# Perceiver kernel: which batches get their keys and values made ahead, and row chains moved to VectorE

## The chip, the cores and the metric

The kernel runs on one core of one Trainium2 chip. The metric is the device time of one execution in microseconds (us); three runs of the kernel before took 1544.31, 1554.78 and 1555.05 us, the median is 1554.78 us.

## What is computed

Two layers over x of 16 batches x 64 rows x 256 columns, all in 32-bit floating point. Each batch also has a context of 1024 positions x 256. Cut to what matters (layer norms have no weights):

```
x = x + cross_attention_0(layernorm(x), ctx)       # 16 heads of 16, keys and values from ctx
x = x + column_attention(layernorm(x))             # across the 16 batches, rotary, softmax with +1
x = x + mixture_of_experts(layernorm(x))           # 8 experts, the best 2, capacity 256
x = x + cross_attention_1(layernorm(x), ctx) + out_b   # with a bias per context position and a mask
x = x + row_attention(layernorm(x)) @ w_proj + b_proj  # among the 64 rows of a batch, rotary
x = x + fp4_linear(silu(fp4_linear(n, w_gate)) * fp4_linear(n, w_up), w_down),  n = layernorm(x)
```

`fp4_linear` rounds both operands, in blocks of 16 along the contracted dimension, to a grid of eight magnitudes: the block's scale is the largest absolute value over 6.

## The kernel before

Rows are held as eight tiles `x[n]` of 128 rows (two batches each). TensorE's order is written out by hand (`manual_schedule`); the order on the other engines and on the DMA queues is set by a scheduler from the dependences and the place in the program.

**Cross-attention** (L307 to L625) runs through 64 *slots* `(b, dt, hf)`: batch b, one of two groups of eight heads, one of two halves of the 1024 keys. At step i of the loop at L590, TensorE does the scores of slot i + 2 (L445, four PSUM banks), then the steps of `project` that are due (L597), the 16 transposes of slot i's exponentials (L475), and the products with the values of slot i - 1 (L489). VectorE adds the mask and takes the minimum (L456), ACT takes the exponential (L467), and both copy the transposes back (L217, L219). PSUM has seven banks for this and one for the output. Between two groups of transposes `advance` (L553) takes every open *row chain* one `yield` further: a chain is a Python generator that does the finishing of a batch (`outputs`, L497, with `project_rows`, L297) and then, in the second layer, `row_attention` (L1220) and `feed_forward` (L1361) of a row tile. A `yield` so decides how much of the other work lies between two steps of a chain in TensorE's order. The queries of the next tile (`queries`, L394) are such a chain too.

**Keys and values** of a batch come from eight steps of `project` (L361): four for the keys (L370), four for the values (L385). In the second layer nine batches, 0 to 8 (`AHEAD = 9`), have them made ahead: `make_ahead` (L636) does the eight steps during the first layer's column attention and experts, where `fill` calls for them, and stores them to DRAM (`kd`, `vd`); the second layer loads them (`load_keys`, L346). The others are projected in the second layer. `due` (L542) places their steps: two in each of the slots 4b - 4 to 4b - 1, or, where the batches on both sides are made ahead (`alone`), one in each of the slots 4b - 6 to 4b + 1. With batches 0 to 8 made ahead no batch is `alone`.

**Layer norm of a row tile** (`layernorm_rows`, L241): statistics, the variance and a first guess of its inverse root are made on VectorE (L244 to L253), three Newton steps of three instructions each on 128x1 and the normalization itself (L256 to L260) on POOL. `project_rows` adds the bias on VectorE (L303) and the sum to `x[n]` on POOL (L304).

**`fp4`** (L883): ACT takes absolute values (L890), VectorE the largest of each block (L893), scales, rounds by adding and subtracting a large power of two, and scales back (L894 to L911). `feed_forward` makes gate and up in two halves of 352 columns (L1376, L1379, L1380), quantizes both halves, transposes (L1391) and multiplies by the down weights (L1405). The last row tile goes through the same steps with nothing beside it.

Of the kernel before, what the change touches and what calls it, by code (L numbers as in the profile page):

```python
# [19 lines left out]
P = 128  # L20
# [7 lines left out]
AHEAD = 9  # L28
# [90 lines left out]
def kernel(ctx: ExitStack, tc: tile.TileContext, a: dict, out: bass.AP):  # L119
# [121 lines left out]
    def layernorm_rows(pool, n, name="xnr"):  # L241

        st = small.tile([P, 6], F32, name="bnst")
        nc.vector.bn_stats(st, x[n])  # L244
        mv = small.tile([P, 2], F32, name="mvr")
        nc.vector.bn_aggr(mv, st)
        va = small.tile([P, 1], F32, name="var")
        nc.vector.tensor_scalar(va, mv[:, 1:2], EPS, None, ALU.add)

        half = small.tile([P, 1], I32, name="half")  # L250
        nc.vector.tensor_scalar(half, va.bitcast(I32), 1, None, ALU.logical_shift_right)
        r = small.tile([P, 1], F32, name="rsd")
        nc.vector.tensor_scalar(r.bitcast(I32), half, -1.0, 1597463007.0, ALU.mult, ALU.add)  # L253
        t = small.tile([P, 1], F32, name="nwt")
        for _ in range(3):
            nc.gpsimd.tensor_scalar(t, r, va, r, ALU.mult, ALU.mult)  # L256
            nc.gpsimd.tensor_scalar(t, t, -0.5, 1.5, ALU.mult, ALU.add)
            nc.gpsimd.tensor_tensor(r, r, t, ALU.mult)
        xn = pool.tile([P, D], F32, name=name)
        made[name] = nc.gpsimd.tensor_scalar(xn, x[n], mv[:, 0:1], r, ALU.subtract, ALU.mult)  # L260
        yield
        yield
        yield
        return xn
# [32 lines left out]
    def project_rows(n, oT, w, bias):  # L297

        pm = bank()
        for c in range(KC):  # L300
            nc.tensor.matmul(pm[:, :D], oT[:, c, :], w[:, c, :], start=(c == 0), stop=(c == KC - 1))  # L301
        t = small.tile([P, D], F32, name="prow")
        nc.vector.tensor_tensor(t, pm[:, :D], bias, ALU.add)  # L303
        nc.gpsimd.tensor_tensor(x[n], x[n], t, ALU.add)  # L304


    def cross_attention(layer, wq, wkv, wo, bq, bk, bv, bo, mask, keep, bias, after, ready, arrive, idle):  # L307
        side = "right" if layer else "left"
        with ExitStack() as st:
# [84 lines left out]
            def queries(n):  # L394
# [3 lines left out]
                xn = yield from layernorm_rows(single, n, "xnq")  # L398
# [98 lines left out]
            def outputs(b):  # L497
# [38 lines left out]
                project_rows(n, oT, wo, rowbias(bo))  # L536
# [99 lines left out]
    def make_ahead(b):  # L636
# [3 lines left out]
        for step in range(8):  # L640
# [27 lines left out]
            if step == 7:  # L668
                load_ahead(b + 2)
# [4 lines left out]
    def load_ahead(b, put=nc.sync.dma_start):  # L674
        if b < AHEAD:
            actx[b] = ahead.tile([P, KC, SK], F32, name="actx")
            put(actx[b], a["ctxT"][b].rearrange("(c p) k -> p c k", p=P))
# [3 lines left out]
    ahead_steps = (None for b in range(AHEAD) for _ in make_ahead(b))  # L681
# [201 lines left out]
    def fp4(pool, dst, src, rows, n, tag, most=None):  # L883

        nb = n // BLK
        most = most or n
        shape = [rows, nb, BLK]
        t = pool.tile([P, most], F32, name=f"t{tag}")[:rows, :n]
        t3 = t.rearrange("p (g k) -> p g k", k=BLK)
        nc.scalar.activation(t, src, AF.Abs)  # L890
        yield
        scl = pool.tile([P, most // BLK], F32, name=f"scl{tag}")[:rows, :nb]
        nc.vector.tensor_reduce(scl, t3, AX.X, ALU.max)  # L893
        nc.vector.tensor_scalar(scl, scl, 1.0 / 6.0, 1e-12, ALU.mult, ALU.max)  # L894
        rsc = pool.tile([P, most // BLK], F32, name=f"rsc{tag}")[:rows, :nb]
# [4 lines left out]
            t3, src.rearrange("p (g k) -> p g k", k=BLK), rsc.unsqueeze(2).to_broadcast(shape), ALU.mult  # L900
# [4 lines left out]
        m = pool.tile([P, most], F32, name=f"m{tag}")[:rows, :n]  # L905
# [257 lines left out]
    def quantize_weights(step, pool):  # L1163
        if step < 4:
# [9 lines left out]
            for _ in fp4(pool, q, raw, PG, n, "w"):  # L1174
                pass
# [11 lines left out]
        elif step < 6:  # L1187
# [4 lines left out]
            for _ in fp4(pool, q, raw, P, NI, "d"):  # L1192
                pass
# [14 lines left out]
    def last_layers(one):  # L1208
# [11 lines left out]
        def row_attention(n, two):  # L1220
            vz = vzs[n % 2]
            xn = yield from layernorm_rows(two, n)
# [134 lines left out]
            project_rows(n, oT, wproj, rowbias("L1_attn_b_proj"))  # L1357
# [3 lines left out]
        def feed_forward(n, two):  # L1361
            tok = slice(n * P, (n + 1) * P)
            xn = yield from layernorm_rows(two, n)
            yield from fp4(one, xn, xn, P, D, "h", NI)
# [5 lines left out]
            for g in range(2):  # L1370
                cols = slice(g * NH, (g + 1) * NH)
                pg = bank()[:, :NH]
                pu = bank()[:, :NH]
                for ps, w in ((pg, wgT), (pu, wuT)):
                    for c in range(KC):
                        nc.tensor.matmul(  # L1376
                            ps, xT[:, c, :], w[:, c, cols], start=(c == 0), stop=(c == KC - 1)
                        )
                nc.scalar.activation(h[:, cols], pg, AF.Silu)  # L1379
                nc.vector.tensor_tensor(h[:, cols], pu, h[:, cols], ALU.mult)  # L1380
            yield
            for g in range(2):
                cols = slice(g * NH, (g + 1) * NH)
                yield from fp4(one, h[:, cols], h[:, cols], P, NH, "h", NI)
            yield
            hT = one.tile([P, NCH, P], F32, name="hT")
            for g in range(0, NCH, 3):
# [12 lines left out]
            yield  # L1400
            yield
            py = bank()[:, :D]
            for j in range(NCH):
                w = min(P, NI - j * P)
                nc.tensor.matmul(py, hT[:w, j, :], wdT[:w, j, :], start=(j == 0), stop=(j == NCH - 1))  # L1405
# [13 lines left out]
    with first_layer:  # L1419
# [11 lines left out]
        with (  # L1431
# [19 lines left out]
            fill(8 * AHEAD)  # L1451
# [61 lines left out]
```

## Time and profile before

| | us |
|---|---|
| runs: lowest, median, highest | 1544.31, 1554.78, 1555.05 |
| profiled execution, its own time | 1553.52 |
| its span, first to last instruction | 1551.8 |
| TensorE busy in the span | 1411.0 (91%) |
| VectorE, ACT, POOL busy | 880.4 (57%), 725.3 (47%), 285.4 (18%) |
| mean granted TensorE clock | 0.942 |

In the lines of the timeline each row has the start in us, the duration in us, engine, line of the kernel, operation, output <- input, the shapes, and in brackets the idle time of the engine before it and what ended that. In the rows of waits: total us, times, longest. In the rows by stage: the stage, its length, busy us (instructions) of TensorE, of its weight loads, of VectorE, ACT and POOL, then the granted TensorE clock as a share of full speed, the DMA engines' mean share, and GB/s. Busy times of TensorE are modelled: instructions overlap, so a busy TensorE is not one at its peak.

### The profile page before, as it was taken

The page shows a single profiled execution, that of the slowest core. Times are in us where ns is not written, and L with a number is a line of the kernel's source. Part 1 is how long each engine was busy: PE and PEld are TensorE (multiplying, and loading weights), DVE is VectorE, ACT ScalarE, POOL GpSimd, SP SyncE. Part 2 cuts the span into 40 slices and gives each one's busy share as a digit, 9 for nine tenths or more (in the row PEclk, how much of TensorE's full clock was granted, in tenths as well). Part 3 has the DMA queues.
Part 4 walks back from the last instruction along what each step waited for, and adds up shares of the span by engine and source line. Part 5 has one row for each costly group of instructions (what it writes and reads, how often), then busy time and mean ns, then how long its engine had stood idle before and what let it go on. Part 6 is the DMA issues. An engine that isn't in the chain of part 4 may idle for free.

```text
span 1551.8 us, 32601 instructions
## 1 busy us (share of the span) xinstructions
PE 1411.0 (91%) x13488; PEld 995.0 (64%) x13488; DVE 880.4 (57%) x2325; ACT 725.3 (47%) x1339; POOL 285.4 (18%) x502
## 2 busy tenths in 40 slices
PE   4999999999999998999999787888899999999754
PEld 2667766676667655768887555565657666666542
DVE  2556665656565533365721265675767675757543
ACT  2555555555555532223221475564656465646321
POOL 4101010000000031013300134241414141311111
PEclk8999999999999999999999798888889999999876
DMA  8111110101000021377774232322101111100000
GB/s 281 59 31 35 32 59 32 35 32 59 31 28 2 35 90 70 105 260 235 234 283 147 90 117 94 118 86 74 57 14 46 46 52 49 42 5 1 5 5 3
DMA packets 53073, 119.48 MB, mean 77 GB/s; under 512 B 4877, under 2 KB 24333, under 8 KB 50621
## 3 DMA queue, kind: packets, MB, share of 16 engines
q1 hardware_dynamic: 48876, 109.93, 21.0%
q0 software_dynamic: 1648, 4.72, 1.1%
q10 hardware_dynamic: 2400, 2.76, 0.5%
q8 instruction: 106, 1.74, 0.5%
q14 instruction: 43, 0.34, 0.1%
HBM read 94.32 MB, written 23.07 MB: 76 GB/s over the span
## 4 chain that ended last, share of the span: by engine, by line
PE 73%; DVE 12%; POOL 4%; ACT 4%; DMA 3%; issue 3%; ACTq 0%; POOLq 0%; DVEq 0%; SPq 0%
PE psw L475 11%; PE psw L385 10%; PE psw L370 9%; PE psw L445 8%; PE pso L489 7%; PE psw L659 4%; PE psw L1085 4%; PE psw L1105 4%; DVE e L456 3%; PE psw L646 3%; ACT e L467 3%; PE psw L1376 2%; PE psw L1405 2%; PE psw L301 2%; DMA kd<-astage 1%
## 5 line engine op out<-in xcount | busy, mean ns | idle before, releaser
L467 ACT ACTIVATE e<-e,mn 128x1024 f32<-128x1024 f32 x256 | 291.1, 1139 | 125.3 <-DVE mn L456 125.3
L475 PEld LDWEIGHTS psw<-consts,e 128*128 128x128 f32 x2048 | 242.6, 144 | 111.6 <-issue 64.3
L475 PE MATMUL psw<-consts,e 128*128 128x128 f32 x2048 | 286.8, 280 | 10.1 <-DVE mn L456 5.7
L456 DVE CUSTOM_DVE_ANT_0 e<-psw,negb,mn 128x512 f32<-128x512 f32 x256 | 177.9, 747 | 180.0 <-PE psw L445 180.0
L456 DVE CUSTOM_DVE_ANT_0 e<-psw,negb 128x512 f32<-128x512 f32 x256 | 162.9, 686 | 87.0 <-PE psw L445 86.8
L219 ACT COPY eT<-psw 128x512 f32<-128x512 f32 x320 | 174.1, 590 | 58.3 <-PE psw L475 57.9
L445 PE MATMUL psw<-kT,qm 32*128 32x512 f32 x1024 | 167.7, 690 | 3.4 <-ACT qm L415 1.8
L489 PE MATMUL pso<-eT,v 128*32 128x128 f32 x4096 | 146.0, 286 | 0.0
L370 PE MATMUL psw<-ctxT,w_L_xattn_Wkv 128*128 128x512 f32 x256 | 125.0, 612 | 11.9 <-DMA ctxT<-in_ctxT_dram 11.9
L217 DVE COPY eT<-psw 128x512 f32<-128x512 f32 x192 | 123.0, 678 | 9.3 <-PE psw L475 9.3
L489 PEld LDWEIGHTS pso<-eT,v 128*32 128x32 f32 x4096 | 109.4, 114 | 28.0 <-issue 25.9
L385 PE MATMUL psw<-w_L_xattn_Wkv,ctxT 128*128 128x256 f32 x512 | 123.6, 385 | 0.0
L385 PEld LDWEIGHTS psw<-w_L_xattn_Wkv,ctxT 128*128 128x128 f32 x512 | 93.0, 190 | 33.7 <-issue 11.9
L370 PEld LDWEIGHTS psw<-ctxT,w_L_xattn_Wkv 128*128 128x128 f32 x256 | 44.3, 192 | 68.4 <-issue 55.1
L219 ACT COPY v<-psw 128x512 f32<-128x512 f32 x46 | 27.0, 588 | 123.8 <-PE psw L385 123.8
L304 POOL TENSOR_TENSOR x<-x,prow 128x256 f32<-128x256 f32 x24 | 17.4, 727 | 315.1 <-DVE prow L303 315.1
L659 PE MATMUL psw<-w_L_xattn_Wkv_w,actx 128*128 128x256 f32 x288 | 73.4, 409 | 0.8 <-ACT astage L653 0.8
L445 PEld LDWEIGHTS psw<-kT,qm 32*128 32x128 f32 x1024 | 49.2, 197 | 37.8 <-issue 20.2
L337 POOL TENSOR_SCALAR negb<-m 128x1024 f32<-128x1024 uint8 x16 | 16.7, 1046 | 285.8 <-DVE mn L456 172.4
L380 ACT ACTIVATE kT<-psw,colb 128x512 f32<-128x512 f32 x48 | 32.8, 687 | 75.3 <-PE psw L370 75.3
L646 PE MATMUL psw<-actx,w_L_xattn_Wkv_w 128*128 128x512 f32 x144 | 66.2, 599 | 1.3 <-DVE x L632 1.3
L659 PEld LDWEIGHTS psw<-w_L_xattn_Wkv_w,actx 128*128 128x128 f32 x288 | 58.0, 206 | 13.6 <-issue 3.8
(248 smaller groups left out, 1974.0 us busy)
## 6 DMA issues: line engine op xcount, KB each, us to landing
ctxT<-in_ctxT_dram SPq DMA_DIRECT2D x23, 1024.0 KB, 5.0
w<-in_L_ffn_w_dram SPq DMA_DIRECT2D x16, 1024.0 KB, 6.9
actx<-in_ctxT_dram SPq DMA_DIRECT2D x9, 1024.0 KB, 6.8
kd<-astage SPq DMA_DIRECT2D x36, 256.0 KB, 3.7
vd<-astage SPq DMA_DIRECT2D x36, 256.0 KB, 2.4
kT<-kd SPq DMA_DIRECT2D x9, 1024.0 KB, 6.1
v<-vd SPq DMA_DIRECT2D x9, 1024.0 KB, 5.0
ab<-in_fside_BxS_dram SPq DMA_DIRECT2D x32, 256.0 KB, 3.4
```

What stands on the lines that cost most here:

```text
L217: nc.vector.tensor_copy(dst, src)
L219: nc.scalar.copy(dst, src)
L370: nc.tensor.matmul(pm, wkv[:, c, dt * P : (dt + 1) * P], ctxT[b][:, c, cols], start=(c == 0), stop=(c == KC - 1),)
L385: nc.tensor.matmul(pm[:, j * D : (j + 1) * D], ctxT[b][:, c, (k + j) * P : (k + j + 1) * P], wkv[:, c, D : 2 * D], start=(c == 0), stop=(c ...
L445: nc.tensor.matmul(sc[g], qm[b // 2][r : r + 32, dt, b % 2, :, :].rearrange("p j q -> p (j q)"), kT[b][r : r + 32, dt, cols], start=True, ...
L456: nc.vector.tensor_tensor_reduce(out=e[:, cols], in0=sc[g], in1=negb[b][:, cols], scale=1.0, scalar=3e38 if hf == 0 else mn[b][:, 0, pr : ...
L467: nc.scalar.activation(e, e, AF.Exp, scale=-1.0, bias=mn[b][:, 1, pr : pr + 1], accum_out=sums[b][:, pr : pr + 1])
L475: nc.tensor.transpose(pt[:, g * P : (g + 1) * P], es[b, dt, g][:, k * P : (k + 1) * P], ident)
L489: nc.tensor.matmul(po[b][32 * g : 32 * g + 32, dt, :], v[b][:, k, pr * 32 : (pr + 1) * 32], e[:, g, :], start=(k == 0), stop=(k == NK - 1),)
L646: nc.tensor.matmul(pm, w1kv[:, c, dt * P : (dt + 1) * P], actx[b][:, c, cols], start=(c == 0), stop=(c == KC - 1),)
L659: nc.tensor.matmul(pm[:, j * D : (j + 1) * D], actx[b][:, c, (k + j) * P : (k + j + 1) * P], w1kv[:, c, D : 2 * D], start=(c == 0), stop=( ...
L1085: nc.tensor.matmul(ph[:, j * CAP : (j + 1) * CAP], w1[:, c, (f + j) * P : (f + j + 1) * P], xeT[:, c, :], start=(c == 0), stop=(c == KC - 1),)
```

## The change

- `AHEAD` lists the nine batches made ahead: 0, 1, 2, 4, 6, 8, 10, 12, 14. So 3, 5, 7, 9, 11, 13 and 15 are projected in the second layer, and each is `alone`. Loads and stores follow the list.
- `layernorm_rows` can do the Newton steps and the normalization on VectorE (two tiny instructions a step instead of three, and one ahead). `row_attention`, `feed_forward` and the first queries of the second layer use that; the other queries stay on POOL. With the argument set, it has no `yield`s of its own.
- In the second layer `x[n]` gets the bias of the coming projection on POOL as soon as it has been normalized, and `project_rows` adds the product to it in one instruction on VectorE.
- `fp4` leaves out the pass on ACT; the maximum takes absolute values itself. Its tiles come from the caller.
- `feed_forward` works in columns 0 to 383 and 384 to 703, with more `yield`s between its steps. For the last row tile there are none, and the second part's gate and up stand behind the first part's scaling; transposes and down products of the first part stand ahead of the quantization of the second.

```diff
-AHEAD = 9
+AHEAD = (0, 1, 2, 4, 6, 8, 10, 12, 14)
...
-    def layernorm_rows(pool, n, name="xnr"):
+    def layernorm_rows(pool, n, name="xnr", vector=False):
...
+        xn = pool.tile([P, D], F32, name=name)
+        if vector:
+            nc.vector.tensor_scalar(va, va, -0.5, None, ALU.mult)
+            for _ in range(3):
+                nc.vector.tensor_scalar(t, r, va, r, ALU.mult, ALU.mult)
+                nc.vector.scalar_tensor_tensor(r, t, 1.5, r, ALU.add, ALU.mult)
+            made[name] = nc.vector.tensor_scalar(xn, x[n], mv[:, 0:1], r, ALU.subtract, ALU.mult)
+            return xn
         for _ in range(3):
             nc.gpsimd.tensor_scalar(t, r, va, r, ALU.mult, ALU.mult)
...
-    def project_rows(n, oT, w, bias):
+    def project_rows(n, oT, w, bias=None):
...
+        if bias is None:
+            nc.vector.tensor_tensor(x[n], pm[:, :D], x[n], ALU.add)
+            return
...
-                xn = yield from layernorm_rows(single, n, "xnq")
+                xn = yield from layernorm_rows(single, n, "xnq", layer == 1 and n == 0)
+                if layer:
+                    nc.gpsimd.tensor_tensor(x[n], x[n], rowbias(bo), ALU.add)
...
-                project_rows(n, oT, wo, rowbias(bo))
+                project_rows(n, oT, wo, None if layer else rowbias(bo))
...
-    ahead_steps = (None for b in range(AHEAD) for _ in make_ahead(b))
+    ahead_steps = (None for i in range(len(AHEAD)) for _ in make_ahead(i))
...
-    def fp4(pool, dst, src, rows, n, tag, most=None):
+    def fp4(tiles, dst, src, rows, n, lo=0):
...
-        nc.scalar.activation(t, src, AF.Abs)
-        yield
-        scl = pool.tile([P, most // BLK], F32, name=f"scl{tag}")[:rows, :nb]
-        nc.vector.tensor_reduce(scl, t3, AX.X, ALU.max)
+        nc.vector.tensor_reduce(scl, s3, AX.X, ALU.max, apply_absolute_value=True)
...
-            xn = yield from layernorm_rows(two, n)
+            xn = yield from layernorm_rows(two, n, "xnr", True)
+            nc.gpsimd.tensor_tensor(x[n], x[n], rowbias("L1_attn_b_proj"), ALU.add)
+            yield
+            yield
             xT = transposed_rows(two, xn)
...
-            project_rows(n, oT, wproj, rowbias("L1_attn_b_proj"))
+            project_rows(n, oT, wproj)
...
+            halves = [slice(0, 3 * P), slice(3 * P, NI)]
+            if alone:
+
+                hidden(halves[0])
+                tiles = fp4_tiles(one, "h", NI)
+                first = fp4(tiles, h[:, halves[0]], h[:, halves[0]], P, 3 * P)
+                next(first)
+                hidden(halves[1])
+                for _ in first:
+                    pass
+                turn_hidden(0)
+                py = bank()[:, :D]
+                down(0)
+                for _ in fp4(tiles, h[:, halves[1]], h[:, halves[1]], P, NI - 3 * P, 3 * P):
+                    pass
+                turn_hidden(3)
+                down(3)
+            else:
+                for cols in halves:
+                    hidden(cols)
+                    yield
+                for cols in halves:
+                    yield from fp4(fp4_tiles(one, "h", NI), h[:, cols], h[:, cols], P, cols.stop - cols.start)
+                yield
+                turn_hidden(0)
+                yield
+                turn_hidden(3)
+                yield
+                yield
+                py = bank()[:, :D]
+                down(0)
+                down(3)
```

Here `hidden` does gate, up, silu and their product for some columns, `turn_hidden` the transposes, `down` three of the six down products; `alone` is true for row tile 7.

## The prediction

> **What bounds the kernel now.** I read the page's slices first: TensorE is busy in nine tenths or more nearly everywhere, but its granted clock falls in two places, slices 22 to 30 and the last three. Both are in the second layer, so I cut that layer into stages at the first score matmul (L445) of every eighth slot; the timeline puts those of slots 16, 24, 32, 40, 48 and 56 at 974.6, 1051.6, 1130.1, 1208.6, 1290.8 and 1372.9. Eight slots are two batches and one tile of rows; I call them a pair.
>
> ```profile
> core 0: us, PE busy (x) PEld busy (x) DVE busy (x) ACT busy (x) POOL busy (x), PEclk, DMA share, GB/s
> 974.50:1051.50 77.00, 66.56 (x676) 45.65 (x668) 53.92 (x153) 43.33 (x83) 24.01 (x43) 0.84 0.25 85
> 1051.50:1130.00 78.50, 66.74 (x676) 45.20 (x668) 51.78 (x147) 42.17 (x81) 24.06 (x43) 0.83 0.20 63
> 1130.00:1208.60 78.60, 75.59 (x741) 51.32 (x734) 54.84 (x153) 45.84 (x87) 23.90 (x43) 0.96 0.11 36
> 1208.60:1290.70 82.10, 79.78 (x768) 55.86 (x764) 55.77 (x155) 46.83 (x89) 23.90 (x43) 1.00 0.15 48
> 1290.70:1372.80 82.10, 79.79 (x771) 55.87 (x764) 55.76 (x155) 46.83 (x89) 21.56 (x41) 1.00 0.11 35
> 1372.80:1444.50 71.70, 67.98 (x670) 48.16 (x662) 49.12 (x137) 40.77 (x76) 10.77 (x25) 1.00 0.01 3
> 1462.50:1551.80 89.30, 42.24 (x284) 27.78 (x272) 36.66 (x102) 15.05 (x29) 14.19 (x36) 0.69 0.01 3
> ```
>
> The reader is to see that a pair without any projection of keys and values (the first two rows) takes 77.0 and 78.5 us, hardly less than one with two projections (82.1), though it has some 95 matmuls fewer. The work saved there is lost again: 11.8 us idle (78.50 - 66.74), and a clock of 0.83. The pairs with two projections are TensorE's own, at clock 1.00 with 2.3 us idle. What TensorE waits for in the second of these rows:
>
> ```profile
> PE psw L301 <- DVE oT L1349: 2.9, 1, 2.9
> PE psw L269 <- POOL xnq L260: 2.5, 1, 2.5
> PE psw L527 <- DVE osb L514: 2.5, 1, 2.5
> PE psw L475 <- DVE mn L456: 1.4, 2, 1.2
> PE psw L1286 <- ACT vz L1276: 1.3, 1, 1.3
> ```
>
> Each row is one wait of the row chains, met because too little other work stands ahead of it in TensorE's fixed order. With two projections a pair, only three are left, of 1.4, 0.5 and 0.4 us. The last 89 us are another stage: row tile 7 alone, a chain of small steps on four engines.
>
> **The change part by part.** The sum is made against the profiled execution: 1553.52 us, of it 1551.8 span and 1.7 around it; the median of the runs, 1554.78, lies 1.3 above.
>
> *Which batches are made ahead.* Nine before, nine after, so the work ahead (L646, L659) and its stores are the same and cost nothing new up to 875.7. In the second layer seven batches are projected in both, but one step in each of slots 6 to 61 instead of two in each of slots 32 to 59. One projection is 16 and 32 matmul records: 7.03 us (L646 x16) and 7.07 us (L659 x32) in the timeline at full clock, 14.1, or 1.76 a step.
>
> A pair will have one projection. Floor: 82.1 - 14.1 = 68.0, TensorE alone. Ceiling: 82.1, since a pair with twice the projection takes no more. Nearest is slots 56 to 63, the only pair with one projection (batch 15): 71.7 at clock 1.00, without the queries of a next tile (8 L405 and 2 L269 matmuls, some 1.5), so 73.2. There all steps stand in the first four slots; spread, they stand ahead of every wait, and the order of the built kernels moves the waiting steps too: four gate and up matmuls (some 2.5 us) now stand between L511 and L527, and a slot's scores and a step between the normalization's sums and L301. That takes off the 2.9 and the two 2.5. VectorE gets more (below). I take 72: five pairs from slot 16 on fall from 398.3 (77.0 + 78.5 + 78.6 + 82.1 + 82.1) to 360, **-38**. Slots 56 to 63 lose two steps of eight, **-3**.
>
> Slots 0 to 15 take 98.8 now, with TensorE busy 82.7 at clock 0.86; ten steps come in, 17.6 us. Idle is 16.1 and the slow clock costs up to 0.14 x 98.8 = 13.8, so between 0 and +17.6; most falls into holes, but the start at 875.7 runs at half clock anyway: **+4**.
>
> [...] In 1051.5 to 1130 the longest idle time is 2.9 us and the clock is 0.83 all the same. [...] I go by the rows: the pairs whose gaps are under 1.5 us have 1.00.
>
> *What queues it passes.* On SP, in the built kernel, a made batch's values are now issued ahead of its keys, and wait for the last use (L489) of the batch three before; the keys then have five slots, against 6.1 us to land (kT<-kd): nothing. Context loads are issued some eight slots ahead: nothing. But the value tile of a projected batch gets the buffer of the batch just before it, so the first value evacuations wait for that batch's last L489, two slots on. Meanwhile up to three of seven PSUM banks are held while four are wanted for scores. No row shows this; below, nothing (the banks come free as scores are read); above, two slots whose transposes go through one bank, each four 0.55 of L475 and 0.6 of copy one after the other: 4.6 instead of 2.0, twice, 5.2 us, plus a stretch at half clock as from 1121.2 to 1128.0, 3.4: 9 a batch. I take 1, inside the 72.
>
> *Chains on VectorE.* Per row tile two Newton chains leave POOL for VectorE: seven tiny instructions at 0.15 and one 128x256 at 0.41 (L234), 1.5 us each, 3 a pair. VectorE goes from 53.8 (between 51.8 and 55.8) to some 57 of 72: not the bound, though its densest slots are near it. Abs on ACT goes (0.42 + 0.49 + 0.48 a tile), the maximum reads the source instead. No row has a maximum with the absolute value in it: between L893's own 0.42 for 128x256 and twice that, two passes; I take L893's own. The six in the weights' quantization lie beside a stage where TensorE is busy 188 of 190 us: nothing either way. The first query's chain: L269 at 871.6 waits for ACT's staging copies, long after xnq is made at 857.1: 0.
>
> *The tail*, where nothing covers:
>
> ```profile
> 1513.40 0.42 DVE L303 TENSOR_TENSOR prow<-psw,rowb 128x256 f32<-128x256 f32 x1 [1.22 <-PE psw L301]
> 1513.90 0.72 POOL L304 TENSOR_TENSOR x<-x,prow 128x256 f32<-128x256 f32 x1 [19.86 <-DVE prow L303]
> 1515.98 0.33 POOL L256 TENSOR_SCALAR nwt<-rsd,var 128x1 f32<-128x1 f32 x1 [1.35 <-DVE rsd L253]
> 1518.96 1.22 POOL L260 TENSOR_SCALAR xnr<-x,mvr,rsd 128x256 f32<-128x256 f32 x1
> 1520.21 0.42 ACT L890 ACTIVATE th<-xnr 128x256 f32<-128x256 f32 x1 [14.65 <-POOL xnr L260]
> 1530.78 0.52 DVE L1380 TENSOR_TENSOR h<-psw,h 128x352 f32<-128x352 f32 x1 [6.44 <-PE psw L1376]
> 1543.44 5.21 PE L1405 MATMUL psw<-wdT,hT 128*128 128x256 f32 x12
> 1548.69 0.42 DVE L1407 TENSOR_TENSOR prow<-psw,x 128x256 f32<-128x256 f32 x1 [6.41 <-PE psw L1405]
> ```
>
> POOL's addition goes from the path twice (tile 7 after each attention), 0.8 each: -1.6. The chain from 1515.86 to 1520.18 is 4.3; seven steps at the 0.19 from L251 to L253 and 0.41 make 1.7: -2.6, twice, -5.2. One Abs: -0.5. The last feed-forward: its first half is ready at 1531.3; with 384 columns some 0.5 later. Quantizing 352 took 1532.37 to 1537.45 with Abs and the other half's product; so 384 end at 1537, 320 at 1541 (4.0), then transposes and copies 1.1 and half of L1405, 2.6: 1544.7 for 1548.7, -4. And L1229 (1486.3) stands behind tile 6's gate and up matmuls though its input was there at 1480.8; in the new order these come ahead of tile 7's transposes while TensorE idles: between 0 and -5.5, I take -3. Together **-14**.
>
> Sum: -38 - 3 + 4 - 14 = -51: span 1501, time **1502**.
>
> **The rivals.**
> *All is covered.* The pair reaches its floor, 68 (340 for five), the first slots cost nothing, the tail gives 20: -58 - 3 - 20 = -81, 1472. For it: clock 1.00 and small gaps as soon as projections are there. Against: VectorE at 57 of 68.
> *The waits stay.* The half of a pair with the feed-forward takes nearly as long without a projection as with one (slots 28 to 31 and 36 to 39, from L445 to L445: 45.2 and 45.7), so its length may be the chains' own; then a pair stays at 78.5: 392.5, -6; the first slots +8, the tail -10: -8, 1545. Against: slots 60 to 63, the same half without projection but at clock 1.00, take some 36 (1409.4 to about 1445).
> *Slower: banks held by values.* The one mechanism is the value evacuation waiting two slots, at seven batches, 9 us each at the upper price: -51 + 63 = +12, 1565. It decides from 7.3 us a batch on (51 / 7, on top of mine). For it: the wait is in the built kernel. Against: four banks remain, and one comes free with each score that VectorE has read, every 0.75 us (L456).
> That the spreading doesn't happen can't be: the built order has one step in each of slots 6 to 61.
>
> **How the numbers follow.** Mine 0.60 (its own range: pairs of 70 to 75, first slots 0 to +8, tail -18 to -10: 1484 to 1526), all covered 0.15, the waits stay 0.14, slower 0.11. The range reaches from 1470 into the first rival to 1545 at the second; it leaves out the slower one and half of the first. A measurement of this kernel can tell about 1% from no change (15.5 us, so 1539 and 1570). Faster by over 1%: 0.60 + 0.15 + 0.05 of the second rival, 0.80. Within 1%: the rest of the second, 0.09, and half of the third, since its 1565 lies under 1570: 0.14. Slower by over 1%: the other half, 0.06.
>
> **What would show it.** Right: pairs of 70 to 75 us from slot 16 on, all alike, clock near 1.00 from slot 8 to 63; no TensorE wait over 1.5 us on oT, osb or xnq; last attention matmul near 1426 instead of 1462; 75 us after it instead of 89. Wrong: a pair still at 78 with clock 0.83 (the waits stay); TensorE waiting at scores or transposes for value copies once in eight slots (banks); VectorE over 0.9 busy in a pair. My number falls if the gaps are not the cause of the slow clock.

## The result, and the profile after

The changed kernel takes 1561.32 us (median of 11 runs, 1558.45 to 1563.77) against 1544.75 for the kernel before (11 runs, 1543.51 to 1555.05): ratio 1.0103, 95% interval 1.0082 to 1.0124. The forecast was 1502. The profiled span is 1558.2 us against 1551.8. The profiled execution of before (1553.52) is one of the slower of its runs, which lie near 1544 and near 1555; so stages of the two profiles differ by 6.4 us in all, the medians by 16.6, and the other 10 can't be placed in a stage.

| stage, us | before | after | difference | forecast |
|---|---|---|---|---|
| slots 0 to 15 | 98.8 | 106.4 | +7.6 | +4 |
| five pairs, slots 16 to 55 | 398.3 | 417.5 | **+19.2** | **-38** |
| slot 56 to the last attention matmul | 90.6 | 87.7 | -2.9 | -3 |
| after it | 88.3 | 69.3 | -19.0 | -14 |

(The second layer also starts 1.3 later.) Over the five pairs TensorE's idle time rises from 30 to 60 us. Its busy time falls from 368 to 358, less than the 14 us of the eight projection steps (of 48) that have moved from here to slots 0 to 15. The rows by stage of the changed kernel, with columns as before; the first is slots 0 to 15, then two pairs, then the tail:

```profile
877.00:983.40 106.40, 91.87 (x904) 63.46 (x904) 64.87 (x191) 68.71 (x130) 29.77 (x42) 0.92 0.23 75
1066.60:1150.70 84.10, 72.58 (x716) 51.30 (x717) 55.14 (x168) 43.48 (x82) 16.43 (x23) 0.90 0.18 59
1150.70:1233.80 83.10, 70.95 (x716) 49.91 (x717) 55.20 (x168) 43.38 (x82) 16.41 (x23) 0.92 0.19 60
1488.90:1558.20 69.30, 38.97 (x244) 25.75 (x244) 39.02 (x118) 12.27 (x23) 3.44 (x4) 0.74 0.01 4
```

The pairs are alike, as forecast, but at 83 to 84 us instead of 72: TensorE idles 11.5 us of 84.1 and has a clock of 0.90. VectorE is busy 55 us of 84, so its total is not what binds. TensorE's waits in the first of the two pairs:

```profile
PE psw L276 <- POOL xnq L267: 5.9, 1, 5.9
PE psw L276 <- DVE xnr L261: 2.8, 1, 2.8
PE psw L1402 <- ACT xTr L278: 2.3, 1, 2.3
```

The waits of before on oT (2.9) and osb (2.5) are gone, as forecast, and the one on vz (1.3) too. The one on the next tile's normalized queries (xnq), 2.5 before and forecast to go as well, is 5.9 now. Two others are new: for the row attention's normalized rows (xnr), and for the transposed rows of gate and up (xTr). Where those on xnq and xnr come from is in the timeline of the same pair, some of VectorE's and POOL's instructions and the two of TensorE that wait:

```profile
1107.33 1.03 PE L308 MATMUL psw<-w_L_xattn_out_w,oT 128*128 128x256 f32 x4
...
1109.55 0.36 DVE L310 TENSOR_TENSOR x<-psw,x 128x256 f32<-128x256 f32 x1
1109.95 0.43 DVE L244 BATCH_NORM_STATS2 bnst<-x 128x6 f32<-128x256 f32 x1
1110.29 0.47 DVE L919 TENSOR_TENSOR th<-h,rsch 128x320 f32<-128x320 f32 x1
...
1113.38 0.74 DVE L468 CUSTOM_DVE_ANT_0 e<-psw,negb,mn 128x512 f32<-128x512 f32 x1
...
1116.42 0.41 DVE L261 TENSOR_SCALAR xnr<-x,mvr,rsd 128x256 f32<-128x256 f32 x1
...
1116.88 0.69 PE L276 MATMUL psw<-consts,xnr 128*128 128x128 f32 x2 [2.78 <-DVE xnr L261]
...
1118.73 0.42 DVE L244 BATCH_NORM_STATS2 bnst<-x 128x6 f32<-128x256 f32 x1
...
1123.03 1.22 POOL L267 TENSOR_SCALAR xnq<-x,mvr,rsd 128x256 f32<-128x256 f32 x1
...
1124.30 0.69 PE L276 MATMUL psw<-consts,xnq 128*128 128x128 f32 x2 [5.88 <-POOL xnq L267]
```

Read it down VectorE's queue. The normalization of xnr starts at 1109.95 and ends at 1116.83: 6.9 us. Between its small steps stand the quantization of the *previous* tile's second half (L919 here, to L930) and the score minima of the slot (L468, 0.74 each). The queries' statistics stand behind all that (1118.73), POOL's chain takes till 1124.25, and TensorE, which has both transposes in the same slot, has nothing else to do: its order is fixed.

### The profile page after: what moved, and what is told of

Same layout as the page of the kernel before. It is cut to its first block, busy times and chain, and to the rows that moved or that the text cites. A ratio compares the mean times of both kernels' runs of the same rounds, so it can differ in the third digit from the quotient of the medians.

```text
span 1558.2 us, 32502 instructions
## 1 busy us (share of the span) xinstructions
PE 1404.6 (90%) x13488; PEld 995.3 (64%) x13488; DVE 896.2 (58%) x2461; ACT 712.3 (46%) x1309; POOL 225.3 (14%) x332
## 4 chain that ended last, share of the span: by engine, by line
PE 73%; DVE 15%; ACT 4%; issue 3%; DMA 2%; POOL 2%; ACTq 0%; SPq 0%; POOLq 0%; DVEq 0%
PE psw L487 11%; PE psw L395 9%; PE psw L380 8%; PE psw L457 8%; PE pso L501 7%; DVE e L468 5%; PE psw L672 4%; PE psw L1104 4%; PE psw L1124 4%; PE psw L659 3%; ACT e L479 3%; PE psw L1402 2%; PE psw L1251 1%; PE psw L1427 1%; PE psw L417 1%
## 5 line engine op out<-in xcount | busy, mean ns | idle before, releaser
L487 PE MATMUL psw<-consts,e 128*128 128x128 f32 x2048 | 281.3, 279 | 6.6 <-ACT e L479 4.3
L468 DVE CUSTOM_DVE_ANT_0 e<-psw,negb,mn 128x512 f32<-128x512 f32 x256 | 178.8, 747 | 158.8 <-PE psw L457 158.8
L468 DVE CUSTOM_DVE_ANT_0 e<-psw,negb 128x512 f32<-128x512 f32 x256 | 163.1, 686 | 121.2 <-PE psw L457 120.6
L219 ACT COPY eT<-psw 128x512 f32<-128x512 f32 x320 | 173.4, 591 | 88.3 <-PE psw L487 88.1
L457 PE MATMUL psw<-kT,qm 32*128 32x512 f32 x1024 | 158.3, 655 | 4.4 <-PE pso L501 2.6
L501 PE MATMUL pso<-eT,v 128*32 128x128 f32 x4096 | 139.4, 278 | 0.0
L380 PE MATMUL psw<-ctxT,w_L_xattn_Wkv 128*128 128x512 f32 x256 | 128.5, 628 | 11.7 <-DMA ctxT<-in_ctxT_dram 11.7
L217 DVE COPY eT<-psw 128x512 f32<-128x512 f32 x192 | 123.2, 681 | 4.4 <-PE psw L487 4.3
L501 PEld LDWEIGHTS pso<-eT,v 128*32 128x32 f32 x4096 | 105.4, 111 | 23.3 <-issue 21.4
L666 ACT ACTIVATE astage<-psw,colb 128x512 f32<-128x512 f32 x36 | 24.6, 687 | 79.2 <-PE psw L659 44.7
```

The source lines that it names most:

```text
L217: nc.vector.tensor_copy(dst, src)
L219: nc.scalar.copy(dst, src)
L380: nc.tensor.matmul(pm, wkv[:, c, dt * P : (dt + 1) * P], ctxT[b][:, c, cols], start=(c == 0), stop=(c == KC - 1),)
L457: nc.tensor.matmul(sc[g], qm[b // 2][r : r + 32, dt, b % 2, :, :].rearrange("p j q -> p (j q)"), kT[b][r : r + 32, dt, cols], start=True, ...
L468: nc.vector.tensor_tensor_reduce(out=e[:, cols], in0=sc[g], in1=negb[b][:, cols], scale=1.0, scalar=3e38 if hf == 0 else mn[b][:, 0, pr : ...
L487: nc.tensor.transpose(pt[:, g * P : (g + 1) * P], es[b, dt, g][:, k * P : (k + 1) * P], ident)
```

## The experiments

Theory W: the new waits make the loss. VectorE gives xnr and xnq late, and the new `yield`s put TensorE's steps ahead of that. Theory S, the first rival: the spread itself costs. The time is the median, the ratio is to the kernel before on the same chip. The runs were on several chips, and beside them the kernel before took from 1544.75 to 1552.96 us; so two kernels are best compared by their ratios. The other columns come from one profile each. "Pair" is the mean of the five in slots 16 to 55.

| kernel | time, us | ratio (95%) | slots 0-15 | pair | 56 to last attention | after it |
|---|---|---|---|---|---|---|
| before | 1544.75 | 1 | 98.8 | 79.7 | 90.6 | 88.3 |
| as changed | 1561.32 | 1.0103 (1.0082 to 1.0124) | 106.4 | 83.5 | 87.7 | 69.3 |
| e1 spread alone | 1560.65 | 1.0101 (1.0067 to 1.0135) | 107.9 | 78.9 | 88.0 | 88.9 |
| e2 first nine | 1556.91 | 1.0056 (1.0028 to 1.0084) | 102.7 | 83.5 | 87.3 | 70.4 |
| e4 Newton on POOL | 1559.09 | 1.0070 (1.0039 to 1.0102) | 104.1 | 82.3 | 92.4 | 72.4 |
| e3 queries on VectorE | 1550.53 | 0.9984 (0.9966 to 1.0002) | 104.4 | 81.7 | 89.6 | 68.8 |
| e5 queries a slot earlier | 1540.50 | 0.9960 (0.9936 to 0.9984) | 108.6 | 78.5 | 91.0 | 68.8 |
| e6 query step later | 1523.63 | 0.9858 (0.9815 to 0.9902) | 105.2 | 76.4 | 87.7 | 68.7 |
| e14 four yields back | 1537.09 | 0.9945 (0.9920 to 0.9971) | 108.7 | 78.6 | 84.6 | 74.0 |
| e11 all yields back | 1525.28 | 0.9840 (0.9808 to 0.9873) | 107.6 | 75.7 | 84.0 | 72.7 |
| e15 all yields back, first nine | 1525.77 | 0.9865 (0.9814 to 0.9916) | 100.8 | 76.4 | 90.1 | 73.2 |
| e8 = e6, first nine | 1528.00 | 0.9874 (0.9820 to 0.9927) | 98.3 | 78.3 | 86.9 | 69.2 |
| e9 = e6, last tile whole | 1524.15 | 0.9849 (0.9799 to 0.9899) | 105.1 | 76.6 | 88.8 | 71.5 |
| e7 = e6, rows later | 1529.11 | 0.9890 (0.9839 to 0.9940) | 102.3 | 78.3 | 82.3 | 75.3 |
| e12 = e6, gate later | 1508.69 | 0.9721 (0.9694 to 0.9747) | 105.3 | 74.6 | 82.0 | 69.4 |
| e10 = e6, rows later twice | 1523.32 | 0.9822 (0.9791 to 0.9853) | 101.3 | 77.1 | 84.3 | 68.7 |
| e13 = e10, products later too | 1504.02 | 0.9725 (0.9674 to 0.9776) | 100.3 | 73.5 | 88.8 | 70.2 |

**The spread alone, and the chains alone (e1, e2).** e1 is the kernel before with the list of batches only; e2 is the changed kernel with batches 0 to 8.

```diff
-AHEAD = 9                                  # e1, on the kernel before
+AHEAD = (0, 1, 2, 4, 6, 8, 10, 12, 14)
...
-AHEAD = (0, 1, 2, 4, 6, 8, 10, 12, 14)     # e2, on the changed kernel
+AHEAD = tuple(range(9))
```

> The kernel before with only the list of batches made ahead taken from the change. Theory W (waits): the spread itself does what was forecast; the changed kernel loses it because VectorE, first in first out, reaches the normalizations xnr and xnq late and TensorE's fixed order waits there (2.8 and 5.9 to 6.5 us a pair). Then this kernel, whose normalizations stay on POOL and whose yields are the old ones, has pairs of about 72 us and takes about 1510 us against 1545. Theory S (spread): one projection step in every slot, with value tiles that hold PSUM banks for two slots, is itself what costs; then pairs of 80 or more here too, with waits at scores or transposes, and 1550 or more.

> The changed kernel with batches 0 to 8 made ahead, as before: the chains alone. Theory W: the waits for xnr and xnq come from VectorE's queue and stay in every pair, with or without projection; pairs without projections take 78 or more, those with two 85 to 90; with the tail 19 us shorter, 1545 to 1560. Theory S: without the spread the pairs are those of before (77 to 82) and the shorter tail shows whole: about 1526.

Both halves cost by themselves, and together no more than the spread alone. e1 refutes W as it stood (pairs of 72, 1510). A pair of it still has, with a projection step in each slot:

```profile
PE psw L527 <- DVE osb L514: 2.5, 1, 2.5
PE psw L301 <- DVE oT L1351: 1.8, 1, 1.8
PE psw L269 <- POOL xnq L260: 0.5, 1, 0.5
```

Against the waits of before (2.5, 2.9, 2.5) the one on xnq nearly goes, the one on oT shrinks, and the one on osb stays in three of the five pairs (1.4 in the other two). S's time came (1550 or more), but not its pairs of 80 or more (78.9 here), nor longer waits at the scores than 1.6 us; what the spread adds lies in slots 0 to 15. e2 hits W: pairs without a projection have 6.1 us on xnq and 5.5 on xnr and take 77 to 79, those with two have 5.0 on xnq and take 89. So the new waits belong to the chains' part of the change.

**Which part of the chains (e4, e6).** e4 puts the three Newton steps and the normalization of tiles 0 to 6 back on POOL and leaves all places in TensorE's order. e6 leaves the engines and moves one place: the transposes of the queries.

```diff
-            xn = yield from layernorm_rows(two, n, "xnr", True)
+            xn = yield from layernorm_rows(two, n, "xnr", True if n == NT - 1 else None)   # e4; None: on POOL, no yields
...
                 if layer:
                     nc.gpsimd.tensor_tensor(x[n], x[n], rowbias(bo), ALU.add)
+                if layer and n:          # e6: one slot later
+                    yield
+                    yield
+                    yield
+                    yield
                 xT = transposed_rows(single, xn, "xTq")
```

> The changed kernel with the Newton chains and the normalization of row tiles 0 to 6 in row_attention and feed_forward on POOL again, its yields unchanged. Theory W in the narrow form (the seven tiny instructions and one 128x256 per chain are what delays VectorE): the wait for xnq falls by about 3 us a pair, 1561 to about 1545. Theory W in the wide form (the place of the normalizations against the quantization, not the engine, makes the wait): xnr comes later by POOL's 4.3 us and the pair doesn't get shorter, 1560 to 1575. Theory S: 1561, no change.

> The changed kernel with four more yields ahead of the transposes of the next tile's queries in the second layer, so that they stand one slot later in TensorE's order; nothing else. Theory W: the wait for xnq (5.9 to 6.5 us a pair) goes, with it the 10 to 14 us at half clock that follow it, which cost 5 to 7; a pair falls from 83.6 to 72 to 76, the time from 1561 to about 1505. Theory S: the pair keeps 83, 1561, and the wait turns up elsewhere.

e4 changes next to nothing, though VectorE has 3.4 us less a pair: waits of 3.5, 2.3 and 2.3 stay. e6 takes 38 us off: no wait on xnq, pairs from 83.5 to 76.4. W's direction, not its size: 2.8 on xnr and 2.3 on xTr are left. Which engine does the row tiles' chains hardly matters here; where a chain's consumer stands does.

**The same wait, tried at its other end (e3, e5).** e3 does all queries' chains on VectorE, with three `yield`s so that their transposes stay where they were; e5 starts them one slot earlier, and their transposes move along.

```diff
-                xn = yield from layernorm_rows(single, n, "xnq", layer == 1 and n == 0)
+                xn = yield from layernorm_rows(single, n, "xnq", layer == 1)    # e3
...
+                if layer and n:                                                 # e3
+                    yield
+                    yield
+                    yield
...
-                    if i % 8 == 2 and i // 8 + 1 < NT:
+                    if i % 8 == (1 if layer else 2) and i // 8 + 1 < NT:        # e5
```

> The changed kernel with the Newton steps and the normalization of all queries on VectorE too, their places in TensorE's order unchanged. Theory W: the statistics still come at the same late point of VectorE's queue, and only POOL's 4.2 us after them go against 3 us or more there, mixed with other work: the wait of 5.9 us falls by 1 to 3, pairs 80 to 83, time 1540 to 1555. Rival (POOL's chain is the lateness): the wait falls below 2 us, pairs 76 to 78, time about 1525.

> The changed kernel, but the next tile's queries start one slot earlier in the second layer; the place of their transposes in TensorE's order moves with them. Theory W (VectorE works its queue in order and reaches the queries' statistics late): if the statistics now come ahead of the last tile's long chain in that queue, the wait of 5.9 us on the queries goes and the time is about 1525, pairs 76. Rival (what counts is the distance in TensorE's order alone, since the start and the transposes move together): the wait stays between 4 and 6 us, pairs 82 to 84, time 1550 to 1560.

e3: the wait falls to 3.6 to 4.1 us and the pairs to 81.7, as W had it; POOL's chain is 2 us of the lateness. e5 lies between the two: 3.0 us on xnq stay and a new wait of 2.0 on xTr comes at the row attention's products.

**Which yields (e11, e14).** With the move, a normalization lost its three `yield`s and got two (row attention) or one (feed-forward) back, and `fp4` lost one with the pass on ACT: four a tile. The two halves got new ones. e14 gives back the four only, e11 restores the halves' places too.

```diff
             nc.gpsimd.tensor_tensor(x[n], x[n], rowbias("L1_attn_b_proj"), ALU.add)
             yield
             yield
+            if not n == NT - 1:          # e14 and e11
+                yield
...
             yield from fp4(fp4_tiles(one, "h", NI), xn, xn, P, D)
             yield
+            if not alone:                # e14 and e11
+                yield
+                yield
+                yield
             xT = transposed_rows(two, xn)
...
                 for cols in halves:      # e11
                     hidden(cols)
-                    yield
+                yield
                 for cols in halves:
+                    yield
                     yield from fp4(fp4_tiles(one, "h", NI), h[:, cols], h[:, cols], P, cols.stop - cols.start)
                 yield
                 turn_hidden(0)
-                yield
                 turn_hidden(3)
```

> The changed kernel with as many yields between the steps of a row tile as before the change (three between a normalization's sums and its transposes, eight up to the gate and up products' input, both halves together), but with its chains on VectorE, without the pass on ACT, with the bias on POOL and the last tile as changed. Theory W (where the steps stand in the fixed order decides, not who does the chain): the wait on the queries falls from 5.9 to at most 2.5 us, as in the kernel with the spread alone (0.5), pairs 76 to 79, time 1520 to 1540. Rival (the chains on VectorE are too long there, wherever they stand): waits on xnr and xnq of 5 us or more, pairs 82 to 84, time 1550 to 1565.

> The changed kernel with only four yields given back, those that the normalization and the quantization of the rows lost with the move to VectorE: one ahead of the row attention's transposes, three ahead of the transposes for gate and up (tiles 0 to 6). Halves, queries, everything else as changed. Theory W, told apart by this: it was the lost yields, which put TensorE's steps ahead of what they need; then the wait on the queries falls to at most 1.5 us and the pairs to 75 to 77, time 1520 to 1530, as with all yields as before (1525.3). Rival (it was the new places of the two halves of gate and up and of their quantization): waits of 4 us or more on the queries stay, pairs 80 to 83, time 1545 or more.

e11 meets W: the ratio falls from 1.0103 to 0.9840, some 40 us. A pair of it, and the waits in it:

```profile
1058.10:1133.00 74.90, 67.98 (x722) 47.31 (x718) 56.58 (x167) 43.20 (x82) 17.36 (x23) 1.00 0.20 66
```

```profile
PE psw L539 <- DVE osb L526: 2.5, 1, 2.5
PE psw L308 <- DVE oT L1373: 1.8, 1, 1.8
PE psw L487 <- DVE eT L217: 1.1, 1, 1.1
PE psw L276 <- POOL xnq L267: 0.9, 1, 0.9
```

TensorE is busy 68.0 us at clock 1.00, what the forecast's floor had for a whole pair; the rest of the 74.9 is the old waits on osb and oT and small ones. With the four yields alone (e14) some 60% of that comes back. It lies between the two theories: the wait on the queries is gone, as W had it, but the pairs take 78.6 and the time is 1537, so the places of the halves count too. The timeline shows what the four yields do:

```profile
1103.21 0.43 DVE L244 BATCH_NORM_STATS2 bnst<-x 128x6 f32<-128x256 f32 x1
...
1106.03 0.41 DVE L261 TENSOR_SCALAR xnr<-x,mvr,rsd 128x256 f32<-128x256 f32 x1
...
1107.63 0.55 DVE L1412 TENSOR_TENSOR h<-psw,h 128x384 f32<-128x384 f32 x1
1108.10 0.41 DVE L244 BATCH_NORM_STATS2 bnst<-x 128x6 f32<-128x256 f32 x1
```

The same normalization takes 3.2 us, start to end, since the previous tile's gate and up products (the first, L1412, at 1107.63) and their quantization now come after it, and the queries' statistics follow 1.7 us behind instead of 1.9 behind a chain of 6.9. The four yields did not only give TensorE other work; they kept the two tiles' chains apart on VectorE.

**What the spread is worth (e15, e8).** e15 is e11, and e8 is e6, with batches 0 to 8 (the second diff above).

> The kernel with yields as before the change (1525.3 us), with batches 0 to 8 made ahead as before the change: the chains' part of the change without the spread and without the lost yields. If the spread is worth what the forecast's stages say (pairs without a projection 72 to 77, with two 82, against 75 alike; first slots 4 to 7 less), five pairs take 385 to 398 against 378.6 and the time is 1527 to 1540. Rival (the spread brings nothing by itself, as the run with it alone said): 1515 to 1526.

> The kernel with the later query step (1523.6 us), with batches 0 to 8 made ahead, as before the change. Theory W (projections spread over all pairs cover waits): the early pairs keep the waits of 5.5, 2.3 and 1.5 us that the changed kernel has with batches 0 to 8, so they take 73 to 76, the late ones 82 to 84: five pairs near 393 against 382, the first slots 2.5 less; time about 1532. Theory S (the spread itself costs): the time is at or under 1515.

0.9865 against e11's 0.9840 and 0.9874 against e6's 0.9858, with intervals that overlap in both: the spread can't be told from nothing here. In the two other pairs of kernels that differ by it alone it costs: 1.0% with the old chains (e1), 0.5% with the chains as changed (e2 and the changed kernel). By the stages of e15 and e11 it takes 3 us off the five pairs (381.9 to 378.6), though eight steps, 14 us of TensorE's work at full clock, have left them, takes 7 off what follows, which has lost two, and adds 7 to slots 0 to 15, where the ten have come in. Length less TensorE's busy time, summed over the five pairs, says why it is so little: in e15 the idle time is 12.5 + 12.1 + 3.5 + 1.1 + 0.8 = 30, much in the pairs without a projection and little in those with two; in e11 it is 6.9 in each pair, 35. One step in each slot shortens the waits of every pair and ends none, where two steps in each slot end them in some pairs. (Before the change the sum is 30 too, with the spread alone 37, as changed 60, in e13 9.) Idle time is not all: e15 has the idle time of the kernel before and the same waits on oT, osb and xnq, and yet its pairs are 16 us shorter, all of it in TensorE's busy time (352 us for 368), with granted clocks of 0.92, 0.88 and 1.00 in the first three pairs for 0.84, 0.83 and 0.96.

**The last tile (e9).** e6 with the halves of the last tile one after the other, as in the others.

```diff
-            alone = n == NT - 1
+            alone = False
```

> The kernel with the later query step (1523.6 us), but the last row tile takes the same steps as the others: both halves of gate and up first, then both quantizations, transposes and down products. Everything before the last attention matmul stays. Forecast's term: 4 us, so the stretch after the last attention matmul is 72 to 73 us instead of 68.7 and the time about 1528. Rival (the gain of 19 us there comes from the normalization chains and the bias taken off the path alone): 68 to 70, the time 1523 to 1525.

The stretch after the last attention matmul grows by 2.8 us, between the forecast's 4 and the rival; the ratios do not differ. By these two profiles the halves are worth some 3 of the 19.

**Covering what is left (e7, e12, e10, e13).** All on e6, for tiles 0 to 5 (e7: 0 to 6): e7 moves the row attention's transposes and the gate and up products two yields later, e12 only the latter; e10 moves the row attention's transposes by one and the ones for gate and up by three, e13 also two steps that e10 still waits at.

```diff
             xT = transposed_rows(two, xn)        # feed_forward
             yield
             yield
+            if n < NT - 2:                       # e12
+                yield
+                yield
...
+            if n < NT - 2:                       # e13, on e10
+                yield
             project_rows(n, oT, wproj)
...
                 yield                            # outputs, ahead of the transposes of osb
                 yield
+                if layer and n < NT - 2:         # e13, on e10
+                    yield
```

> The kernel with the later query step (1523.6 us), and also two yields more between the normalization of a row tile and its transposes ahead of the row attention, and two more between the transposes and the gate and up products (not for the last tile). Theory W: the waits of 2.8 us (xnr) and 2.3 us (xTr) a pair go, and the stretches at half clock behind them (clock now 0.94 to 0.98): pairs of 76 fall to 70 to 72, the time to about 1500. Rival (the chain is as long as its steps; what is moved later only meets the next wait): pairs stay at 75 to 77, the time between 1515 and 1530.

> The kernel with the later query step (1523.6 us), and only the gate and up products two yields later after their transposes (tiles 0 to 5). Theory W: the wait of 2.3 us on xTr goes and nothing takes its place: pairs 73 to 74.5, time 1510 to 1516. Rival (the steps behind it move too and meet other waits): pairs 75.5 to 78, time 1520 to 1530.

> The kernel with the later query step (1523.6 us), with one yield more ahead of the row attention's transposes and three more ahead of the transposes for gate and up (tiles 0 to 5), so that both stand as far behind their sums as before the change. Theory W: the wait on xnr (2.8 us) falls to 1 or less and the one on the quantized rows that came up when only the first was moved (5.9) stays away: pairs 72 to 74, time 1503 to 1512. Rival: another wait of 3 us or more a pair takes the place, pairs 76 or more, time at or over 1523.

> The kernel with the later query step and both row steps later (1523.3 us), and one yield more ahead of the two steps that its pairs still wait at: the transposes of a batch's finished rows (osb 2.5 us) and the row attention's projection (oT 1.8 us), tiles 0 to 5. Forecast's claim, put to the test: with the waits covered a pair takes 72; so the pairs of 75.2 to 78.4 fall to 70 to 73, the time to 1493 to 1505. Rival (each step moved later meets another wait): pairs 75 or more, time 1515 to 1530.

e7 is the rival's: 2.8 and 2.3 go, and a wait of 5.9 comes, on the quantized rows (xnr L935), whose transposes stand as few steps behind their normalization as before; with three yields there (e10) it is gone. e12 gains 1.4% over e6 with two yields: pairs 74.6, longest wait 1.8. e10 is the rival's too: xnr is no longer waited for, but osb (2.5) and oT (1.8) are, as with the old yields. e13 covers those as well: 1504.02, 2.7% under the kernel before and, with e12, the best of these kernels; the time is in the range that the forecast's claim gave, the pairs of 73.5 just above theirs. A pair of e13 and its longest waits:

```profile
1197.60:1270.90 73.30, 71.02 (x720) 49.05 (x716) 57.69 (x168) 43.36 (x82) 16.59 (x23) 1.00 0.20 67
```

```profile
PE psw L308 <- DVE oT L550: 0.8, 1, 0.8
PE psw L492 <- DVE mn L473: 0.6, 1, 0.6
```

Its idle time is 2.3 us where e11's pair has 6.9, at the same clock, but it is only 1.6 shorter: TensorE's busy time is 71.0 instead of 68.0. The eight score matmuls of a slot, 1.14 us from start to end in all eight slots of e11's pair, take 1.8 to 2.9 in three slots of this one. In the longest of them their weight loads wait 0.9 us for VectorE's copy of a key tile out of PSUM (kT, L388) and 0.3 for one of transposes (eT, L217). So a part of the waits has moved into what counts as busy.

## Why the prediction was wrong

- **The step that failed** is "I take 72", with its reason "spread, they stand ahead of every wait, and the order of the built kernels moves the waiting steps too. That takes off the 2.9 and the two 2.5". Two of those three waits did go (oT, osb); the one on xnq grew from 2.5 to 5.9, two new ones came (2.8, 2.3), and the term, -38, came out at +19. Nor does one step a slot stand ahead of every wait by itself: with the spread alone (e1) osb keeps 2.5 or 1.4 and oT 1.8, and the five pairs take 394. I looked at what the order does to the old waits and not at what it does to every other step with an input.
- **Under it lies a second one**: "seven tiny instructions at 0.15 and one 128x256 at 0.41 (L234), 1.5 us each, 3 a pair". As busy time that holds (VectorE 55.1 us a pair). As delay it doesn't: alone in the queue such a chain takes 2.1 us from its first to its last step (e14), and here two tiles' chains shared VectorE's queue, and the normalization took 6.9 us from start to end, 3.2 where they stood apart (e14). "Its densest slots are near it" saw the place and set no price on it.
- **The yields were priced at nothing.** With the four lost ones back (e14) the ratio is 0.016 lower, with the places of the halves as before too (e11) 0.026, some 40 us, with the same batches, engines and instructions in the chains. That undoes the loss, but it is not yet the forecast: e11 is 1.6% under the kernel before, about half of the 51 us.
- **The spread** is worth about nothing where the chains' steps stand well (e11 to e15, e6 to e8), and costs 0.5 to 1.0% where they don't (e2, e1), instead of 38 + 3 less 4. "They stand ahead of every wait" took one step of 1.8 us to be as good as the pairs with two steps a slot, whose waits were gone. It shortens each wait and leaves the idle time's sum as it was (35 us against 30).
- **72 as such was near**: with no wait over 0.8 us a pair takes 73.3 (e13; five of them 367, forecast 360). That it is not the floor of 68 is in part the scores' own waits for copies out of PSUM, for which the sum had 1 us a batch (for copies of values).
- **Slots 0 to 15**: +7.6 for +4. "Most falls into holes" did not hold: TensorE's idle time only fell from 16.1 to 14.5. That ten steps of 17.6 us cost no more is in its busy time, which grew by 9.2 (82.7 to 91.9), with the clock at 0.92 instead of 0.86. Waits on xnq are 8.9 us there, and were 7.2. With the queries' step and both row steps later (e10, e13) the stage falls to 101.3 and 100.3, +2.5 and +1.5.
- **Slots 56 to the last attention matmul**: -2.9 for -3. **The tail**: -19.0 for -14. From the last attention matmul to the row attention's projection (48.7 before, 37.1 after) I had -6.4 and it gave -11.6. All of the -6.4 lies ahead of the row attention's first products, which come 14.6 us after the last attention matmul instead of 22.8: -8.2. If the addition and the chain gave their -3.4, -4.8 is left for the gate and up products of tile 6, in "between 0 and -5.5", of which I took -3. The other -3.4 had no term: tile 6's down products stood behind the transposed weights of the row attention, and now stand ahead of them, where TensorE would wait for the softmax. From the projection on I had -7.9, and it gave -7.3.
- **The rivals.** None happened. "All is covered" and "the waits stay" both took the list of waits as given. No wait for value copies is in the list of the pair: the rival with the banks had a mechanism of the built kernel and no cost that the list shows. Waits of scores for copies out of PSUM were found in e13, for keys and transposes.
- **What the gaps do to the clock.** I went by "the pairs whose gaps are under 1.5 us have 1.00". That was read from the rows of before, and is no rule: e11 has 1.00 with gaps of 2.5, and in e12 half clock followed a gap of 1.8. See the last section.

## What to carry to other kernels

Where one engine's order is fixed by hand, a move of work between engines is first a change of when each consumer's input is there: list, for every step of the fixed order, what it needs and how late that now is, not only the waits that the old profile shows. A `yield` (or any filler between producer and consumer) that goes with the removed instruction has to be given back on purpose, and the delay of a chain of small steps is read from its start and end in a full queue, not from the sum of its durations. Work that is spread out evenly to cover waits shortens many instead of ending some, and the idle time's sum need not fall.

## What the runs showed of the hardware

Gaps of one length were followed by different granted clocks. In e10 and e11 TensorE waits equally long for osb in a pair, 2.48 us. Timeline of e10, and its rows for the wait itself and for the stretch from 1.6 us after it on (the granted clock is the number after POOL's):

```profile
1087.20 0.44 PE L544 MATMUL psw<-consts,osb 128*128 128x128 f32 x2 [2.48 <-DVE osb L531]
```

```profile
1084.70:1087.20 2.50, 0.02 (x2) 0.00 (x1) 2.42 (x5) 2.50 (x6) 2.34 (x3) 1.00 0.60 252
1088.80:1092.20 3.40, 3.40 (x12) 1.63 (x9) 1.58 (x5) 0.00 (x0) 0.00 (x0) 0.50 0.57 160
```

Timeline of e11, the same wait:

```profile
1088.37 0.44 PE L539 MATMUL psw<-consts,osb 128*128 128x128 f32 x2 [2.48 <-DVE osb L526]
```

and its row right after it:

```profile
1088.50:1092.00 3.50, 3.50 (x47) 2.25 (x48) 1.79 (x6) 0.95 (x3) 1.08 (x1) 1.00 0.46 155
```

Half clock for 3.4 us after the one (0.50), full clock in the 3.5 us after the other, and all through e11's pair (1.00 in its row above) with gaps of 2.5, 1.8 and 1.1 us. In e12 a gap of 1.8 us, up to 1085.45, was followed by 3.4 us at 0.50, from 1086.40 to 1089.80. What tells these cases apart was not shown.

So pairs of the same work differ by clock as well, and a few us in the stage table are of this kind: two of e10's five pairs take 75.3 and 75.2 us at clock 1.00, the other three 78.4 to 78.5 at 0.96.
